# Row directions first in image 0, and a quarter of its front as side steps of its first scans

## The chip, the cores and the metric

The kernel runs on one core of one Trainium2 chip. A core has five engines that are programmed apart from each other: TensorE (PE, with its weight loads as PEld), VectorE (DVE), ScalarE (ACT), GpSimd (POOL) and SyncE (SP), which here issues all transfers between the chip's memory and the core's on-chip buffers; sixteen DMA engines carry them out. The metric is the device time of one launch in microseconds, the median of the runs. Beside it stands one execution taken by the hardware profiler, with the start and the duration of every instruction.

## The reference, cut to what matters

Eight images of 96 channels and 64 x 64 pixels go through a state-space block and an attention block. What concerns this change is the first half of the first block:

```
xn = _ln(shortcut, ln1_w, ln1_b)
xz = jnp.einsum('bhwc,ec->bhwe', xn, in_proj_w)
xw, z = jnp.split(xz, 2, axis=-1)
xc = lax.conv_general_dilated(xc, conv_w, (1, 1), 'SAME', ...)      # 3x3, by channel, 192 channels
xc = _silu(xc + conv_b[None, :, None, None])
s0 = _local_scan(xc, WSZ, False)                                    # 8x8 windows, row by row
s1 = _local_scan(xc, WSZ, True)                                     # the same, column by column
xs = jnp.stack([s0, s1, s0[..., ::-1], s1[..., ::-1]], axis=1)      # four directions
x_dbl = jnp.einsum('bkdl,kcd->bkcl', xs, x_proj_w)                  # step sizes, B and C of each direction
...
def step(hst, inp):
    dA = jnp.exp(dt_i[..., None] * A)
    hst = dA * hst + (dt_i * u_i)[..., None] * b_i[:, :, None, :]
    y = jnp.einsum('bkdn,bkn->bkd', hst, c_i)
```

The scan runs over all 4096 pixels of an image, once in each of four directions: rows forward, rows backward, columns forward, columns backward. Their four outputs are brought back to one order of pixels and added. Norms, gating, two more convolutions, attention and a small feed-forward part follow (the back end).

## The kernel before, in words

An image is cut into NC = 8 chunks of T = 512 pixels. A chunk holds eight rows of the picture, which is one row of 8 x 8 windows.

**The front** (`front`, line 403) makes what the scans read. It has two stages. `normed` (line 415) takes one chunk at a time: layer norm of the input, written to the scratch tensor `xnd`. `paired` (line 451) takes two neighbouring chunks at a time: it loads 18 rows of `xnd` (`im`), makes z with a silu (written to `zd`), the skip part (`base`), the 3 x 3 convolution as nine products a row block (line 435, 27 steps for a pair), a second silu, and writes the result twice: `u[0]` in the order of rows and `u[1]` in the order of columns (line 505 transposes within windows). Last come the products for step sizes, B and C (`xdbl`, lines 513 and 514), written to `xd[0]` and `xd[1]` in the same two orders. In the column order a chunk of pixels touches all eight column chunks, so the first column chunk is whole only when all four pairs are done; in the row order a chunk is whole when its own pair is.

Each stage works on a kit (`front_kit`, line 300), a set of tiles with a PSUM bank of its own. A stage is a generator: between two `yield`s it issues a few instructions, and the number yielded says after how many steps of the kernel's own clock it wants to go on. `side_by_side` (line 844) runs a stage on several kits by turns, each kit with its share of the chunks. For image 0 this is done before anything else, with four kits (f0, f1, y01, y2): line 877.

**The scans.** A unit is one chunk in one direction: 8 images x 4 directions x 8 chunks = 256 units (lines 855 to 868). In each image the pair of column directions (1) comes first, forward and then backward, and then the row directions (0). A unit has 24 slots. In a slot DVE runs one `tensor_tensor_scan` over 128 x 512 (line 1133) and, in 14 of the 24, a product with C (line 1135); ACT makes the decay for two slots ahead (line 1072) and keeps the carry (lines 1136, 1141); POOL makes the inputs (`inputs`, line 952) and multiplies outputs by C (`outputs`, line 958); PE sums over the states (`sums`, line 972). `plan` (line 1007) says in which slot each of these is issued, and also when the loads for coming units are issued on SP: step sizes two units ahead (`fetched_dt`), B and C (`states`), u, and the spreading of delta and du. `gather` (line 993) takes a unit's sum out of PSUM and asks for its write to `y`; a unit reads, in `before` (line 964), what the direction ahead of it has left there. The first direction reads `u` in its place. Going from the column to the row directions, the backward column units write through a transposing copy (line 999) into `y[0]`.

Every engine works through its own queue in the order of issue, and so does SP. Writes are not issued at once: `later` (line 113) holds a request for three steps of the clock.

**Side streams.** While the units of image b run, one step of a side stream may be issued in each slot (`advance`, line 1096). There are two: the front of image b + 1 on kit_f (PSUM bank f0, at a pace of 1.55 slots for each step), and the back end of image b − 1 on kit_b (bank f1, pace 1). While image 0 runs there is no back end, and bank f1 is idle. The back end's first stage, `gated`, takes a chunk only when it is in the image's `done` set, which `gather` fills as the last direction finishes chunk by chunk. Steps that load another function table on ACT wait for slots in which they disturb least (`quiet`, line 392). Before the units of a new image start, the side streams are run to their end (`drained`).

Of the kernel before, what the change touches and what calls it, by code (L numbers as in the profile page):

```python
# [23 lines left out]
NC = L // T  # L24
# [19 lines left out]
def kernel(ctx: ExitStack, tc: tile.TileContext, a, out):  # L44
# [255 lines left out]
    def front_kit(pool, tag):  # L300
        k = Kit()
        k.tag, k.turn = tag, 0
        k.x = [Part(plain(pool, f"{tag}x{i}")) for i in range(2)]
        k.e = [plain(pool, f"{tag}e{i}") for i in range(4)]
        k.pre = pool.tile([P, 3, T], F32, name=tag + "pre")
        k.im = Part(pool.tile([C + 1, 18, W2], F32, name=tag + "im"))
        k.pad = padded(pool, tag + "pad")
        return k
# [535 lines left out]
    def side_by_side(stages, kits):  # L844

        for stage, cs in stages:
            todo = [cs] if cs is None else [cs[i :: len(kits)] for i in range(len(kits))]
            drained(*(Stream(stage(k, c)) for k, c in zip(kits, todo)))
            drained(Stream(settled()))
# [4 lines left out]

    units, images = [], []
    for b in range(out.shape[0]):
        s = {"b": b, "done": set(), "live": b + 1 == out.shape[0]}
        images.append(s)
        for pair in (1, 0):
            for back in range(2):  # L860
                for i in range(NC):
                    u = Unit()
                    u.s, u.pair, u.back, u.k = s, pair, back, pair + 2 * back
                    u.c, u.start = (NC - 1 - i if back else i), i == 0
                    u.new, u.i = (pair, back, i) == (1, 0, 0), len(units)
                    u.bc, u.hb, u.delta, u.du = {}, {}, {}, {}
                    u.banked = BANKED[int(b == 0 or u.i % 32 >= NC)]
                    units.append(u)

    TILES = [(g, j) for g in range(2) for j in range(3)]  # L870

    fp = ctx.enter_context(tc.tile_pool(name="small", bufs=1))
    kit_f = front_kit(wp, "f0")
    first = front(0, images[0])
    with tc.tile_pool(name="begin", bufs=1) as pool:
        table("natural_log_exp_and_others")
        side_by_side(first, [kit_f] + [front_kit(pool, t) for t in ("f1", "y01", "y2")])

    kit_b = back_kit(wp, "f1", False)
    scan_pool = ExitStack()  # L880
    sp = scan_pool.enter_context(tc.tile_pool(name="scan", bufs=2))

# [80 lines left out]

    def before(u):

        src = u.s["u"][1] if u.k == 1 else u.s["y"][u.pair]
        u.plain = []
        for i, rows in enumerate((slice(0, P), slice(P, src.shape[0]))):
            t = sp.tile([P, T], F32, tag=f"u{i}", name=f"u{i}", bufs=1)[: rows.stop - rows.start]
            u.plain.append(into(t, src[rows, bass.ts(u.c, T)]))  # L970

    def sums(u, ns, m):

        if ns[0] == 0 and m == 0:
            u.p = (bank("y01", "p01"), bank("y2", "p2"))
        low, up = slice(0, 64), slice(64, P)
        if len(ns) == 2:
            todo = [(u.p[0][low], ns[0], m), (u.p[0][up], ns[1], m)]
        else:
            todo = [(u.p[1][low], ns[0], 2 * m), (u.p[1][up], ns[0], 2 * m + 1)]  # L980
        for ps, n, i in todo:
            nc.tensor.matmul(  # L982
                ps, halves, u.hb[n][:, i, :], start=TILES[n][0] == 0 and m == 0, stop=False, skip_group_check=True
            )
        if ns[-1] == 5 and m == 1:
            first = u.k == 1
            for ps, w, x in (
                (u.p[0], dd_a if first else ident, u.plain[0]),
                (u.p[1][low] if first else u.p[1], dd_b if first else ident, u.plain[1]),
            ):  # L990
                nc.tensor.matmul(ps, w, x, start=False, stop=True, skip_group_check=True)  # L991

    def gather(u, i):

        ps, d = u.p[i], slice(P * i, P * i + P)
        t = sp.tile([ps.shape[0], T], F32, tag=f"yt{i}", name="yt", bufs=1)
        dst = u.s["y"][1 if u.k == 1 else 0][d]
        if u.k == 3:
            nc.scalar.copy(transposed(t), scanned(ps))
            later(to_columns(dst, u.c), by_window(t))  # L1000
        else:
            nc.scalar.copy(t, ps)
            later(dst[:, bass.ts(u.c, T)], t)
        if u.k == 2 and i == 1:
            u.s["done"].add(u.c)

    def plan(u, last, nxt, third):

# [93 lines left out]
    for u in units:  # L1102
        last, nxt, third = (at_index(u.i + d) for d in (-1, 1, 2))
        if u.new:
            drained(*side)
            b = u.s["b"]
            side = []
            if b:
                side.append(Stream(chain((SETTLE,), in_turn(back_end(b - 1, last.s), kit_b, False))))
            if b + 1 < out.shape[0]:  # L1110
                side.append(Stream(in_turn(front(b + 1, images[b + 1]), kit_f, True), PACE))
            else:
                final = back_end(b, u.s)
                last_kit = back_kit(None, "f0", True, kit_f)
                side.append(Stream(final[0][0](last_kit, range(1, NC)[::-1])))
        if third and third.new:
            drained(*side[-1:])
            all_issued()
        if u.start:
            carry = sp.tile([P, 24], F32, tag="carry", name="carry")  # L1120
        todo = plan(u, last, nxt, third)
        for slot in range(24):
            n, m = divmod(slot, G)
            g, j = TILES[n]
            q, hb, first_at = 24 * u.i + slot, u.hb[n], 0 if u.back else T - 1
            col = carry[:, 8 * j + g * G + m : 8 * j + g * G + m + 1]
            while kept:
                kept.pop(0)()
            decays(q + 2)
            d = da.pop(q)  # L1130
            banked = m < u.banked[n]
            dd, x = (d[:, ::-1], hb[:, m, ::-1]) if u.back else (d, hb[:, m, :])
            nc.vector.tensor_tensor_scan(dd if banked else x, dd, x, 0.0 if u.start else col, ALU.mult, ALU.add)  # L1133
            if banked:
                nc.vector.tensor_tensor(hb[:, m, :], d, u.bc[1, g][:, m, :], ALU.mult)  # L1135
                kept.append(lambda col=col, d=d, at=first_at: nc.scalar.copy(col, d[:, at : at + 1]))  # L1136
            elif m == G - 1:
                lo = 8 * j + g * G
                kept.append(
                    lambda c=carry[:, lo + u.banked[n] : lo + G].unsqueeze(2), h=hb[:, u.banked[n] :, :], at=first_at:  # L1140
                    nc.scalar.copy(c, h[:, :, at : at + 1])  # L1141
                )
            for f, args in todo[slot]:
                f(*args)
            place[0] = slot
            advance(slot)
# [89 lines left out]
```

## Time and profile before

| What | us |
|---|---|
| Median of 3 runs (11326.49 to 11333.61) | 11327.45 |
| Profiled execution, its own time | 11335.55 |
| Its span, first to last instruction | 11333.8 |
| First scan of image 0 starts | 352.6 |
| First scan of image 1 starts | 1640.4 |
| Busy over the span: DVE, POOL, PE, ACT | 10390.3, 10398.8, 8544.5, 7478.7 |

An answer on stretches of time gives, for each stretch, its length, the busy time and the number of instructions (in brackets) of PE, PEld, DVE, ACT and POOL, the share of full clock that PE was granted, the busy share of the DMA engines and what they moved in GB/s. A line of a timeline gives start, length, engine, source line, operation, the tile written and the tile read, the shapes, and how long the engine had been idle and for whom it had waited. SPq is SP's queue: there the length is that of the issue, not of the transfer. "x2" joins two instructions of one kind that follow each other; a product in 32-bit floats appears as two passes.

### The profile page before, as it was taken

To read this page: it belongs to the slowest core of one execution; us is meant where nothing else is said; L and a number is where in the kernel's file an instruction comes from. 1 tells how busy PE (TensorE), PEld (TensorE's weight loads), DVE (VectorE), ACT (ScalarE), POOL (GpSimd) and SP (SyncE) were. 2 spreads that over 40 slices of the span, in tenths; PEclk is the share of its full clock that TensorE was granted. 3 is DMA by queue.
4 is the path that set the end of the run, shared out by engine and by line. 5 is a ranking of instruction groups with operands and counts; after the bars stand their busy time and mean duration, and the time that the engine had idled before them with its cause. 6 is when DMAs were issued, how large, how long until landed. Compare 5 with 4: busy or idle time off the path is not lost. (4 is left out here: it accounts for less than half of the span.)

```text
span 11333.8 us, 97039 instructions
## 1 busy us (share of the span) xinstructions
PE 8544.5 (75%) x23270; PEld 2320.9 (20%) x23270; DVE 10390.3 (92%) x10868; ACT 7478.7 (66%) x14899; POOL 10398.8 (92%) x2783
## 2 busy tenths in 40 slices
PE   6577658887678876888678876788768877676677
PEld 2111112222122211222112221222212221111212
DVE  0799999999999999999999999999999999999993
ACT  3566656767666676667766676666766667666674
POOL 0799999999999999999999999999999999999991
PEclk8678878888788877889788887888878888787788
DMA  2788878898888888888888888889888888888883
GB/s 70 170 197 197 200 188 210 208 226 200 202 207 211 221 198 201 212 212 216 195 212 207 214 217 195 208 205 224 213 197 207 211 220 201 195 199 196 202 199 90
DMA packets 1081040, 2253.25 MB, mean 199 GB/s; under 512 B 419609, under 2 KB 420314, under 8 KB 949395
## 3 DMA queue, kind: packets, MB, share of 16 engines
q1 hardware_dynamic: 1080467, 2247.05, 81.5%
q8 instruction: 184, 3.01, 0.1%
q14 instruction: 389, 3.19, 0.1%
HBM read 1507.14 MB, written 336.69 MB: 163 GB/s over the span
## 5 line engine op out<-in xcount | busy, mean ns | idle before, releaser
L956 POOL TENSOR_TENSOR hb<-b,du 128x2048 f32<-128x2048 f32 x1536 | 6935.8, 4532 | 23.0 <-DMA du<-ua 16.0
L1072 ACT ACTIVATE da<-delta,w_a_logs 128x512 f32<-128x512 f32 x6144 | 4216.4, 689 | 696.7 <-DVE hb L1133 575.6
L982 PE MATMUL p<-hb,halves 128*64 128x512 f32 x12288 | 3813.9, 729 | 809.0 <-POOL hb L962 391.7
L1133 DVE TENSOR_TENSOR_SCAN da<-da,carry,hb 128x512 f32<-128x512 f32 x3087 | 3949.2, 1279 | 57.1 <-ACT da L1072 53.4
L962 POOL TENSOR_TENSOR hb<-hb,c 128x2048 f32<-128x2048 f32 (+2 forms) x768 | 2982.3, 3883 | 304.7 <-ACT carry L1141 262.6
L1133 DVE TENSOR_TENSOR_SCAN hb<-da,carry,hb 128x512 f32<-128x512 f32 x2289 | 2781.1, 1264 | 59.4 <-ACT da L1072 58.4
L1135 DVE TENSOR_TENSOR hb<-da,c 128x512 f32<-128x512 f32 x3528 | 2440.6, 692 | 153.9 <-DVE da L1133 0.9
L1136 ACT COPY carry<-da 128x1 f32<-128x1 f32 x3528 | 554.8, 157 | 2356.0 <-DVE hb L1135 2345.5
L982 PEld LDWEIGHTS p<-hb,halves 128*64 128x64 f32 x12288 | 914.5, 161 | 3556.5 <-issue 2126.2
L435 PE MATMUL conv<-f0im,taps 97*128 97x512 f32 (+1 forms) x2088 | 909.3, 669 | 89.8 <-ACT f0pre L491 50.3
L1133 DVE TENSOR_TENSOR_SCAN da<-da,hb 128x512 f32<-128x512 f32 x441 | 537.8, 1219 | 27.9 <-POOL hb L956 26.5
L938 POOL TENSOR_TENSOR ua<-nat,ua 128x512 f32<-128x512 f32 x256 | 326.7, 1276 | 257.6 <-DMA b<-xd 257.6
L935 DVE SCALAR_TENSOR_TENSOR nat<-dt,nat 128x512 f32<-128x512 f32 x384 | 259.5, 676 | 239.3 <-ACT nat L933 239.3
L921 PE MATMUL dt<-dts,dt_w 7*64 7x512 f32 (+1 forms) x1024 | 450.8, 660 | 18.8 <-DVE nat L935 14.3
L991 PE MATMUL p<-u,ident 128*128 128x512 f32 x768 | 436.0, 695 | 5.3 <-DMA u<-y 5.1
L376 PE MATMUL ctr<-f1b,cen_c 96*96 96x512 f32 x460 | 271.0, 695 | 198.8 <-DVE f1b L770 160.6
L435 PEld LDWEIGHTS conv<-f0im,taps 97*128 97x128 f32 (+1 forms) x2088 | 254.5, 175 | 676.4 <-issue 524.4
L1133 DVE TENSOR_TENSOR_SCAN hb<-da,hb 128x512 f32<-128x512 f32 x327 | 377.9, 1204 | 4.9 <-ACT da L1072 4.9
L382 PE MATMUL var<-f1b,ones_c 96*96 96x512 f32 x346 | 207.9, 685 | 152.6 <-ACT f1b L379 143.0
L1141 ACT COPY carry<-hb 128x4 f32<-128x4 f32 (+2 forms) x768 | 146.7, 191 | 197.3 <-DVE hb L1133 184.8
L656 PE MATMUL cab<-f1m,cab_w 96*96 96x512 f32 x348 | 206.0, 719 | 91.1 <-ACT f1b L665 41.7
L619 PE MATMUL cab<-f1im,cab_w 97*32 97x512 f32 x1044 | 264.7, 627 | 12.8 <-DMA f1im<-xld 7.9
(425 smaller groups left out, 7479.0 us busy)
## 6 DMA issues: line engine op xcount, KB each, us to landing
b<-xd SPq DMA_DIRECT2D x1024, 512.0 KB
c<-xd SPq DMA_DIRECT2D x1024, 512.0 KB
delta<-nat SPq DMA_DIRECT2D x1536, 128.0 KB
du<-ua SPq DMA_DIRECT2D x1024, 128.0 KB
y<-yt SPq DMA_DIRECT2D x512, 256.0 KB
u<-y SPq DMA_DIRECT2D x384, 256.0 KB
ua<-u SPq DMA_DIRECT2D x256, 256.0 KB
du<-ub SPq DMA_DIRECT2D x512, 128.0 KB
```

The source lines that it names most:

```text
L376: nc.tensor.matmul(ps, cen_c, src, start=i == 0, stop=i == len(srcs) - 1)
L435: nc.tensor.matmul(ps, taps[:, t, lo : lo + n], im[:, r0 + dy : r0 + dy + 8, dx : dx + HW], start=t == 0, stop=t == 8,)
L921: nc.tensor.matmul(ps, dt_w[32 * w.k : 32 * w.k + R + 1, d], w.dts, start=True, stop=True)
L938: nc.gpsimd.tensor_tensor(x, u.nat, x, ALU.mult)
L956: nc.gpsimd.tensor_tensor(hb, u.bc[0, g], u.du[j].unsqueeze(1).to_broadcast([P, G, T]), ALU.mult)
L962: nc.gpsimd.tensor_tensor(hb, hb, u.bc[1, TILES[n][0]][:, lo:, :], ALU.mult)
L982: nc.tensor.matmul(ps, halves, u.hb[n][:, i, :], start=TILES[n][0] == 0 and m == 0, stop=False, skip_group_check=True)
L991: nc.tensor.matmul(ps, w, x, start=False, stop=True, skip_group_check=True)
L1072: nc.scalar.activation(da[q], u.delta[j], AF.Exp, scale=a_neg[:, u.k, j, g * G + m : g * G + m + 1])
L1133: nc.vector.tensor_tensor_scan(dd if banked else x, dd, x, 0.0 if u.start else col, ALU.mult, ALU.add)
L1135: nc.vector.tensor_tensor(hb[:, m, :], d, u.bc[1, g][:, m, :], ALU.mult)
L1136: kept.append(lambda col=col, d=d, at=first_at: nc.scalar.copy(col, d[:, at : at + 1]))
```

## The change

Three things are changed, all for image 0 alone.

The order of its directions is turned: rows forward, rows backward, columns forward, columns backward. `u.order` counts the directions of an image from 0 to 3 and takes the place of tests on `u.k`. The copy into the other order of pixels now stands in the second direction (rows backward write into `y[1]`) and in the fourth (columns backward write into `y[0]`). Since a column chunk touches all chunks, image 0's chunks are declared done all at once, at the gather of its last unit.

The paired stage before the scans takes only the first three pairs of chunks (0 to 5), on three kits. The `normed` stage still takes all eight chunks on four kits; the fourth, kit_2, now lies in the pool that stays, and after the first units kit_b uses its tiles in place of tiles of its own.

The fourth pair (chunks 6 and 7) becomes a side stream on kit_2 while the first units of image 0 run, beside the front of image 1. Before unit 4 it is run to its end, if it has not got there.

```diff
-        s = {"b": b, "done": set(), "live": b + 1 == out.shape[0]}
+
+        s = {"b": b, "done": set(), "live": b + 1 == out.shape[0], "pairs": (1, 0) if b else (0, 1)}
...
+        for order, (pair, back) in enumerate((p, k) for p in s["pairs"] for k in range(2)):
...
-    kit_f = front_kit(wp, "f0")
+    kit_f, kit_2 = front_kit(wp, "f0"), front_kit(wp, "f1")
     first = front(0, images[0])
     with tc.tile_pool(name="begin", bufs=1) as pool:
         table("natural_log_exp_and_others")
-        side_by_side(first, [kit_f] + [front_kit(pool, t) for t in ("f1", "y01", "y2")])
-
-    kit_b = back_kit(wp, "f1", False)
+        kits = [kit_f] + [front_kit(pool, t) for t in ("y01", "y2")]
+        (stage, cs), (behind, pairs) = first
+        side_by_side(((stage, cs),), kits + [kit_2])
+        side_by_side(((behind, pairs[:3]),), kits)
+
+    kit_b = back_kit(wp, "f1", False, kit_2)
...
-        src = u.s["u"][1] if u.k == 1 else u.s["y"][u.pair]
+        src = u.s["y" if u.order else "u"][u.pair]
...
-        dst = u.s["y"][1 if u.k == 1 else 0][d]
-        if u.k == 3:
+
+        other = (u.pair, 1 - u.pair, u.pair, 0)[u.order]
+        dst = u.s["y"][other][d]
+        if other != u.pair:
             nc.scalar.copy(transposed(t), scanned(ps))
             later(to_columns(dst, u.c), by_window(t))
...
-        if u.k == 2 and i == 1:
-            u.s["done"].add(u.c)
+        if u.order == 3 and i == 1:
+            if other == u.pair:
+                u.s["done"].add(u.c)
+            elif u.c == (0 if u.back else NC - 1):
+                u.s["done"].update(range(NC))
...
-            if b:
+            if b == 0:
+                side.append(Stream(behind(kit_2, pairs[3:])))
+            else:
                 side.append(Stream(chain((SETTLE,), in_turn(back_end(b - 1, last.s), kit_b, False))))
...
+        if u.i == pairs[3] - 2:
+            drained(side[0])
         if third and third.new:
             drained(*side[-1:])
```

## The prediction

> **What bounds the kernel now.** I read the page, then busy time by stage, then the timelines of the opening, then busy time by unit.
>
> ```profile
> span 11333.8 us, 97039 instructions
> PE 8544.5 (75%) x23270; PEld 2320.9 (20%) x23270; DVE 10390.3 (92%) x10868; ACT 7478.7 (66%) x14899; POOL 10398.8 (92%) x2783
> ```
>
> DVE and POOL bound the span as a whole, but the page's first slice shows them idle. Busy time by stage (stretch, length, busy us of PE, PEld, DVE, ACT, POOL, clock, DMA share, GB/s):
>
> ```profile
> 147.50:240.50 93.00, 92.89 (x288) 37.02 (x287) 0.00 (x0) 8.04 (x13) 0.00 (x0) 1.00 0.02 6
> 270.20:317.20 47.00, 46.23 (x48) 8.14 (x48) 0.00 (x0) 8.43 (x16) 0.00 (x0) 0.50 0.45 110
> 317.20:352.60 35.40, 6.11 (x8) 1.30 (x9) 1.38 (x2) 7.57 (x12) 7.05 (x4) 0.50 0.85 202
> 352.60:1640.40 1287.80, 855.34 (x2248) 228.26 (x2248) 1252.93 (x1272) 798.05 (x1631) 1280.40 (x336) 0.77 0.81 194
> ```
>
> To 317 us the front of image 0 is bound by PE (93 us of convolution at full clock, 47 us of xdbl products at half clock); then come 35 us of loads; from the first scan at 352.6 us image 0 is bound by POOL (1280 of 1288) with DVE beside it, and PE and ACT have room. Work that leaves the opening and needs only PE, ACT and DMA is a candidate gain.
>
> The opening's timeline on ACT, PE and SP (start, length, engine, line, what):
>
> ```profile
> 242.44 1.48 ACT L443 ACTIVATE f0pre<-f0pre 128x1536 f32<-128x1536 f32 x1
> 246.52 1.48 ACT L443 ACTIVATE f1pre<-f1pre 128x1536 f32<-128x1536 f32 x1
> ```
> ```profile
> 270.25 2.00 PE L513 MATMUL xdbl<-f0pre,xp_a 128*80 128x512 f32 x2 [10.12 <-ACT f0e L521]
> 272.18 1.99 PE L514 MATMUL xdbl<-f0pre,xp_b 64*80 64x512 f32 x2
> 274.10 1.99 PE L513 MATMUL xdbl<-f1pre,xp_a 128*80 128x512 f32 x2
> ```
> ```profile
> 317.18 0.30 SPq L121 DMA_DIRECT2D xd<-y2e  x1
> 319.44 0.61 SPq L896 DMA_DIRECT2D dts<-xd  x2
> ```
>
> A silu costs each kit 4.08 us of ACT (two table loads with it), an xdbl set 3.85 us of PE, and SP stands 2 us at the first dts load.
>
> Busy time of the first four units of image 0, and of one unit of image 1, where two side streams run:
>
> ```profile
> 352.60:391.10 38.50, 19.79 (x44) 4.70 (x46) 38.01 (x41) 21.14 (x45) 38.50 (x10) 0.60 0.67 157
> 391.10:432.30 41.20, 28.52 (x74) 6.94 (x70) 40.59 (x44) 27.05 (x58) 41.20 (x12) 0.79 0.77 186
> 432.30:473.00 40.70, 23.31 (x62) 5.62 (x62) 39.97 (x43) 26.25 (x57) 40.70 (x11) 0.82 0.80 192
> 473.00:514.60 41.60, 26.66 (x70) 6.55 (x68) 40.66 (x43) 27.13 (x58) 40.58 (x12) 0.77 0.80 190
> 1678.00:1725.00 47.00, 40.65 (x98) 9.67 (x94) 43.05 (x46) 31.67 (x66) 44.18 (x12) 0.78 0.91 224
> ```
>
> In the first four POOL is busy almost throughout and PE 98 of 162 us. The crowded unit has PE at 86%, and both DVE and POOL lose time: there lies the risk.
>
> **What the Trainium skill says.** TensorE: Matmul & The Clock Gate, "Part 1: The HAM clock gate": the array runs at half clock until some 3.4 us of sustained activity. The trace agrees for the convolution, but the xdbl products kept PE busy 46 of 47 us and stayed at 0.50, so I don't count on a rise there. ScalarE: Activation LUTs, "What ACT_TABLE_LOAD costs": about 1.28 us for the load itself, plus a drain; the trace has 1.28 us, and 4.08 us from one silu to the next.[...]
>
> **The change, part by part.** Removed from the opening: one of four kits in every round of the paired stage (three chunk pairs on three kits). The normed stage keeps four kits.
> - z: the fourth first product (105.97 − 102.78 = 3.2 us) and a quarter of two rounds (107.80 to 116.16, 2.1 us) make 5.3; with cold and warm rounds mixed otherwise I take 4.5 (3.3 to 5.3).
> - silu on z: 4.1.
> - base: rounds from 132.98 to 147.23, a quarter is 3.6.
> - convolution: 147.23 to 240.4, a quarter is 23.3.
> - silu on u: 4.1.
> - column copies: 3 × 1.01 = 3.0 (L505; the xdbl round behind them waits for ACT).
> - xdbl: 12 sets become 9 after 270 us, 3 × 3.85 = 11.6.
> - dts: with rows first, unit 0 reads what kit f0 wrote some rounds earlier, not the last column write of xd, so SP's stop goes: 2.0 (0 to 2).
> Sum 56.2. The 35 us of loads behind it move whole: b and c are issued after the last xd write and move 202 GB/s either way.
>
> Added to image 0's scans: the front of chunks 6 and 7 on kit_2, one step a slot. Its steps are 93 slots of unit 0 to 3 (11 for landing, 9 z, 10 with silu, 8 base, 33 convolution, 2 and 20 after it, up to 12 of quiet waits), so it is over before unit 4 calls for it at slot 96, and that drain costs nothing; unit 6's dts is fetched just after.
> - PE: 44 matmuls' worth (z 3, base 6, convolution 27, xdbl 8), 0.86 us each at full clock (93.1 us / 108) = 38 us. The four units' 98.3 us at clock 0.75 are 73 us at full clock; 111 of 162 fit above clock 0.69.
> - ACT: 3 × 0.6 + 2 × 4.1 + 2 × 0.6 + 3 × 0.7 + 3 × 1.1 + 4 × 0.6 = 19 us, against 102 busy of 162. The decays queue behind these; units of image 0 in which a silu runs show DVE idle 1.6 to 2.2 us against 0.6 to 0.9, so 1 us each, 2 in all.
> - DMA: im, x, zd, base, both u and xd add about 4.2 MB, 26 GB/s over four units on 157 to 192; units at 207 to 216 GB/s (720 to 800 us) still take 40 to 41 us. On SP each write waits for ACT with the next unit's delta, du, b and c behind it; those are issued 9 or more slots (15 us) ahead. Hidden while steps lag less than that.
> - Stalls from a fuller PE (an eviction on ACT waits, decays behind it): no row gives it for this mix. At best 0; at worst the crowded units' excess DVE idle, at most 3.5 us a unit, 14. I take 4, for the two convolution units.
> So side work costs 6 (2 to 16).
>
> Moved: the direction pairs of image 0. Scans, sums and gathers are as many as before. The transposing gathers now stand in orders 1 and 3, so 16 more copies take 1.09 instead of 0.58 us, and their y writes go in 256-byte runs; ACT has the room: 0 (0 to 2). Chunks of image 0 count as done only after its last gather; but the side stream of image 1 starts at slot 12, after that gather's slot 11, as it does now. Its first y load then stands on SP for a y write issued just before: 2 to 4 us, which SP has free there (1663.5 to 1665.6 is idle) and b's lead covers the rest: 0. kit_b takes kit_2's tiles when the front no longer needs them: 0.
>
> Net 56.2 − 6 = 50. On the profiled execution 11335.6 − 50 = 11285 (its span 11333.8 and 1.8 around it); the median of the runs lies 8.1 below it: 11327.5 − 50 = 11277.
>
> **Rivals.** (a) Full clock in xdbl: with a shorter burst before it, PE may keep its clock. 9 sets × (3.85 − 1.72) = 19 more: 11258. Against: the 3.6 us of idle PE behind the convolution (240.4 to 244.0), where the clock fell, stays, and 9 us of column copies follow. (b) Crowded units: side steps cost as in image 1, 14 to 16: 11287. For it: units at 45 to 47 us there; against: those also carry more DVE work, 43 against 40 us. (c) Slower: the clock stays at half through units 0 to 3. PE needs 111 / 0.5 = 222 us in 162; its lag of 60 us holds the evictions on ACT, and with them decays and DVE: −56 + 60 + 6 = +10, 11338. It decides from a clock under about 0.52; before, those units have 0.60 to 0.82, and this very convolution ran at 1.00. (d) The opening is bound by transfers anyway, and the steps taken out change nothing: 11327. Against: DMA share 0.02 and 0.45 in the two PE stretches.
>
> **From numbers to chances.** Likeliest case 0.70 (own range 11268 to 11288, from the bounds of z, dts and the stalls); (a) 0.10; (b) 0.15, tail to 11300; (c) 0.03; (d) 0.02. The range 11255 to 11298 holds the first, most of (a) and (b). A difference under 0.2% (23 us) can hardly be told from none: faster 0.95, same 0.04 (c, d), slower 0.01 (c with more lag behind it).
>
> **What would show it.** The first scan near 296 us, 56 earlier; convolution 70 us long with three kits; 9 xdbl sets 3.85 us apart (1.7 would be a); dts directly behind the last xd issue. Units 0 to 3 together 162 + 6; DVE idle up by 1 to 2 us a unit, PE over 85% of them. From image 1 on every unit as before. Wrong if the first scan comes as forecast and units 0 to 3 grow by over 16 us, or if image 1's first units grow, where the late "done" would be the cause.

## The result, and the profile after

The changed kernel takes 11288.08 us, median of 5 runs (11276.69 to 11299.44); the kernel before took 11327.45 beside it (11322.44 to 11333.61). The ratio is 0.9964, with an interval of 0.9951 to 0.9976. A second sample on another chip gave 11278.56 (11275.63 to 11292.27) against 11334.86, a ratio of 0.9956 (0.9943 to 0.9968). The forecast was 11277 with a range of 11255 to 11298. The profiled execution was the quickest of the first sample, 11276.69 (forecast for it: 11285).

The page of the changed kernel, span and busy time:

```profile
span 11274.7 us, 97032 instructions
PE 8525.3 (76%) x23270; PEld 2313.7 (21%) x23270; DVE 10391.9 (92%) x10868; ACT 7482.6 (66%) x14899; POOL 10398.6 (92%) x2782
```

DVE and POOL are busy as long as before (10390.3 and 10398.8) and PE nearly so (8544.5); it is the span around them that is shorter. Busy time by stage of the changed kernel: convolution of the opening, last nine xdbl sets, loads, and the units of image 0 (columns as in the prediction: stretch, length, PE, PEld, DVE, ACT, POOL, clock, DMA share, GB/s):

```profile
137.00:206.00 69.00, 68.94 (x215) 27.37 (x213) 0.00 (x0) 5.51 (x9) 0.00 (x0) 1.00 0.01 5
228.50:264.10 35.60, 34.69 (x36) 6.11 (x36) 0.00 (x0) 6.32 (x12) 0.00 (x0) 0.50 0.43 106
264.10:299.20 35.10, 6.11 (x8) 1.28 (x8) 1.43 (x3) 7.57 (x12) 7.10 (x4) 0.50 0.89 208
299.20:1592.10 1292.90, 890.42 (x2356) 241.00 (x2356) 1253.59 (x1273) 820.57 (x1652) 1280.93 (x336) 0.78 0.82 196
```

Convolution and xdbl have each lost a quarter, the loads are as long as before, the first scan starts at 299.2 instead of 352.6, and image 0 takes 5.1 us more. The opening's timelines on ACT, PE and SP, changed kernel:

```profile
207.98 1.48 ACT L443 ACTIVATE f0pre<-f0pre 128x1536 f32<-128x1536 f32 x1
212.07 1.48 ACT L443 ACTIVATE y01pre<-y01pre 128x1536 f32<-128x1536 f32 x1
```
```profile
228.67 2.00 PE L513 MATMUL xdbl<-f0pre,xp_a 128*80 128x512 f32 x2 [7.08 <-ACT f0e L521]
230.60 1.99 PE L514 MATMUL xdbl<-f0pre,xp_b 64*80 64x512 f32 x2
232.52 2.00 PE L513 MATMUL xdbl<-y01pre,xp_a 128*80 128x512 f32 x2
```
```profile
264.05 0.30 SPq L121 DMA_DIRECT2D xd<-y2e  x1
264.40 1.13 SPq L899 DMA_DIRECT2D dts<-xd  x2
266.36 0.35 SPq L906 DMA_DIRECT2D ua<-u  x1
267.92 1.23 SPq L893 DMA_DIRECT2D b<-xd  x2
```

A silu still costs 4.09 us a kit, an xdbl set 3.85 us at half clock. The first dts load stands directly behind the last xd write, as forecast; a stop on SP, 0.8 us long, is now at the load behind it (264.40 + 1.13 = 265.53, and ua at 266.36).

The first four units of image 0 in the changed kernel:

```profile
299.20:337.60 38.40, 22.45 (x54) 5.45 (x56) 37.92 (x41) 22.52 (x48) 38.40 (x10) 0.67 0.75 176
337.60:379.10 41.50, 38.91 (x92) 9.92 (x88) 40.76 (x43) 32.02 (x64) 41.50 (x12) 0.88 0.81 200
379.10:419.80 40.70, 36.69 (x125) 10.36 (x126) 39.96 (x42) 27.51 (x59) 40.70 (x11) 1.00 0.83 206
419.80:464.30 44.50, 33.85 (x90) 7.82 (x86) 40.95 (x44) 35.84 (x68) 40.65 (x12) 0.81 0.85 220
```

Units 1 and 2, which carry the moved convolution, have PE busy for 94% and 90% of their time and are hardly longer than before (41.2 and 40.7). Only unit 3 has grown clearly, from 41.6 to 44.5. What happens there is on DVE and ACT (timelines of the changed kernel; the bracket is the idle time and who ended it):

```profile
429.48 0.68 DVE L424 TENSOR_TENSOR f0pad<-f0e,var 96x512 f32<-96x512 f32 x1 [1.00 <-ACT var L370]
447.99 0.68 DVE L424 TENSOR_TENSOR f0pad<-f0e,var 96x512 f32<-96x512 f32 x1 [1.81 <-ACT var L370]
```
```profile
421.46 1.28 ACT L398 ACT_TABLE_LOAD   x1
422.75 1.48 ACT L443 ACTIVATE f1pre<-f1pre 128x1536 f32<-128x1536 f32 x1
424.25 1.28 ACT L398 ACT_TABLE_LOAD   x1
...
427.18 1.11 ACT L505 COPY f1e<-f1pre 128x512 f32<-128x512 f32 x1
428.19 0.65 ACT L369 ACTIVATE var<-var,eps 96x512 f32<-96x512 f32 x1
428.87 0.57 ACT L370 ACTIVATE var<-var 96x512 f32<-96x512 f32 x1
...
446.24 0.56 ACT L518 COPY f1e<-xdbl 80x512 f32<-80x512 f32 x1
446.70 0.65 ACT L369 ACTIVATE var<-var,eps 96x512 f32<-96x512 f32 x1
447.38 0.57 ACT L370 ACTIVATE var<-var 96x512 f32<-96x512 f32 x1
```

f1 is the moved quarter, f0 the front of image 1. The quarter's silu, with its two table loads, and a column copy (L505) stand on ACT ahead of the two activations of image 1's layer norm (L369, L370). Their consumer on DVE, L424, comes next in DVE's queue, which runs in order: DVE stands for 1.00 us, with the scans behind it. The second stop, 1.81 us where the kernel before has 0.33, comes 18 us later, when the silu is long over. This time copies of the quarter's xdbl results (L518 above, another at 440.12) and the step sizes of a coming unit stand ahead of the norm; that these copies make the difference is read from ACT's order, not tested. DVE's idle time in this unit is 3.55 us, 0.94 in the kernel before.

Span against span: the first scan comes 53.4 us earlier, image 0 grows by 5.1, images 1 to 7 are 7.0 shorter in sum and the end behind the last scan 3.7 shorter, 59.0 in all. Only the first two can be put down to the change. Images 3 to 6 take between 1343 and 1350 us each from one kernel of this study to the next, the tail 240 to 247, though no kernel touches them. The second sample's profile has the first scan at 304.9, image 0 at 1293.1, and a span of 11287.9.

### The profile page after: what moved, and what is told of

Its sections match the earlier page's. It is cut to its first block, busy times and chain, and to the rows that moved or that the text cites. A ratio compares the mean times of both kernels' runs of the same rounds, so it can differ in the third digit from the quotient of the medians.

```text
span 11274.7 us, 97032 instructions
## 1 busy us (share of the span) xinstructions
PE 8525.3 (76%) x23270; PEld 2313.7 (21%) x23270; DVE 10391.9 (92%) x10868; ACT 7482.6 (66%) x14899; POOL 10398.6 (92%) x2782
## 5 line engine op out<-in xcount | busy, mean ns | idle before, releaser
L376 PE MATMUL ctr<-f1e,cen_c 96*96 96x512 f32 x402 | 234.7, 693 | 137.4 <-DVE f1e L770 98.6
L382 PE MATMUL var<-f1e,ones_c 96*96 96x512 f32 x350 | 210.8, 687 | 146.3 <-ACT f1e L379 131.7
```

## The experiments

No kernel leaves a part of the computation out. Some do more: one computes chunks 6 and 7 twice, two give xdbl wider weights, and the four filled ones issue products that nothing reads. A diff is against the changed kernel, in 8, 9, 11 and 12 against the experiment that is carried on; "..." marks lines left out.

**1. The order alone.** All four pairs before the scans, no side stream, only the order of the directions turned.

```diff
-        side_by_side(((behind, pairs[:3]),), kits)
+        side_by_side(((behind, pairs),), kits + [kit_2])
...
-            if b == 0:
-                side.append(Stream(behind(kit_2, pairs[3:])))
-            else:
+            if b:
...
-        if u.i == pairs[3] - 2:
-            drained(side[0])
```

> The directions of image 0 turned, and nothing else: all four pairs of the front before the scans on four kits, no side front. My theory: turning the order is worth almost nothing by itself. SP's 2 us stop at the first dts load goes, but the loads of B and C behind it last as long, so the first scan starts at 351 to 352.5 us (352.6 before); the transposing gathers in the last eight units of image 0 cost 1 to 2 us in image 0, which lasts 1289 to 1290 us (1287.8 before). Device time within 4 us of before. Rival: the turned order is a gain or a loss of its own, through earlier loads (first scan before 348 us) or through the late mark of done chunks (units 0 to 3 of image 1 longer by more than 2 us together).

Measured: 11324.39 us (13 runs) against 11330.84 (26 runs), ratio 0.9997 (0.9988 to 1.0005). First scan at 352.1 (before: 352.6), image 0 1288.9 us (1287.8), the first four units of image 1 37.9, 45.6, 44.4 and 43.6 us, before 37.9, 46.7, 44.7 and 43.6. SP's queue in this kernel:

```profile
317.91 0.30 SPq L121 DMA_DIRECT2D xd<-f1e  x1
318.27 0.82 SPq L899 DMA_DIRECT2D dts<-xd  x2
319.26 0.35 SPq L906 DMA_DIRECT2D ua<-u  x1
```

The stop in front of dts is gone, yet from the last xd write to the first scan 34.1 us pass instead of 35.4: 0.7 of the 2 us are lost again in the loads that follow. The turned order by itself can't be told from no change, and the late "done" costs image 1 nothing.

**2. The side work alone.** The order and the side stream as in the change, but the opening also does all four pairs; the quarter is computed twice.

```diff
-        side_by_side(((behind, pairs[:3]),), kits)
+        side_by_side(((behind, pairs),), kits + [kit_2])
```

> As the changed kernel, but all four pairs are also computed before the scans on four kits; the side stream then computes the front of chunks 6 and 7 a second time, to the same values. So the opening is as long as before and the side work is there: the price of the side work alone. My theory, from the changed kernel's trace: about 3 us in units 0 to 4, nearly all in unit 3 (44 us instead of 41.6), units 1 and 2 as before although PE is filled there, and 1 to 2 us in the last eight units; first scan at 351 to 352.5 us, device time 3 to 8 us above before. Rival, as predicted blind: 6 us in units 0 to 3 with most of it in the convolution's units 1 and 2. Rival of the crowded units: 14 us.

Measured: 11335.62 us (13 runs), ratio 1.0002 (0.9994 to 1.0010). Image 0 takes 1293.0 us, 4.1 more than with the order alone; the first five units are 38.4, 41.6, 40.7, 44.4 and 41.0, as in the changed kernel. So the side work costs 4 us with the long opening as with the short one, and the rest of the change is what the opening loses. The medians of the two kernels lie 11 us apart, with intervals that overlap.

**3. The changed kernel again**, with no edit, as a second sample.

> The changed kernel once more, with more executions than its first comparison had. Its profiled execution was 59 us under before, its median 39. The stages say 53 us less up to the first scan and 5 us more in image 0, so 48. Theory: 48 is what the change does, and the rest is scatter between executions in images 1 to 7; a larger sample gives a ratio of 0.9955 to 0.9962 (43 to 51 us). Rival: the profile's images 3 to 7 (11 us shorter) belong to the change: 0.9950 or less.

Its time is given above. Its ratio lies in the range of the theory, but the interval doesn't shut the rival's 0.9950 out. Its units are 38.4, 41.7, 40.7, 44.4 and 41.0: unit 3 is no accident of one execution. But its first scan stands 5.7 us later. Busy time in one stretch of the base stage, first in the changed kernel's profile, then in that of the second sample:

```profile
119.60:136.00 16.40, 13.83 (x31) 4.48 (x31) 0.00 (x0) 8.63 (x10) 0.00 (x0) 1.00 0.43 137
```
```profile
119.60:136.00 16.40, 15.69 (x18) 4.39 (x18) 0.00 (x0) 7.86 (x8) 0.00 (x0) 0.50 0.43 136
```

One program, two executions: full clock from 119.6 us in one, only from 136.0 in the other, where PE was busy for 96% of these 16 us. That is where the 5.7 us are.

**4. Image 1's front held back.** If unit 3 suffers from two fronts on one ACT, it should recover when image 1's front starts later, at a quicker pace.

```diff
-                side.append(Stream(in_turn(front(b + 1, images[b + 1]), kit_f, True), PACE))
+                ahead = in_turn(front(b + 1, images[b + 1]), kit_f, True)
+                side.append(Stream(chain((68,), ahead), 1.4) if b == 0 else Stream(ahead, PACE))
```

> As the changed kernel, but the front of image 1 waits for 95 slots, until the side front of chunks 6 and 7 is done, and then goes at 1.4 slots a step instead of 1.55, so that it ends in time. It tells what unit 3 of the changed kernel pays for (44.4 us, 41.6 before). Theory: two streams meet; DVE, in its own order, stands at the norm product of image 1's front, which waits for its two ACT functions, which stand behind the silu and the column copies of the side front. Then without that norm unit 3 takes 41 to 42 us and DVE is idle under 1.8 us in it, and units 0 to 2 are 1 to 2 us shorter together (no norm product on DVE). Rival: the silu and the column copies alone hold the decays; unit 3 stays at 43.5 us or more. Device time 0 to 6 us below the changed kernel's in the first case, unless the quicker front costs that later.

Measured: 11286.69 us (4 runs), ratio 0.9962 (0.9948 to 0.9976). Unit 3 of this kernel:

```profile
421.90:463.70 41.80, 33.87 (x84) 7.63 (x80) 39.76 (x42) 31.48 (x60) 41.80 (x12) 0.75 0.88 221
```

Unit 3 falls from 44.4 to 41.8, with POOL busy throughout; DVE's idle time falls from 3.55 to 2.04, not quite to what was expected. Units 0 to 3 take 159.5 us, against 165.0 with both fronts in them and 162.0 in the kernel before, which has only image 1's. So the quarter alone is no dearer than image 1's front alone: either leaves unit 3 at 41.6 to 41.8, both together make it 44.4. That they meet on ACT is what the timelines above show. These sums alone would also fit two costs that merely add, since no kernel has neither front in these units. The held front gives the gain back later (image 0: 1293.8), so this is a diagnosis, no cure.

**5. and 6. Wider products in xdbl.** The xdbl products use 80 columns of the array and, every second one, 64 rows. If the number of columns kept the clock at half, 128 of them should lift it (the 64 rows stay as they are): once padded with zeros (the first two added lines in the loop), once with copies of real columns (the next two, in their place).

```diff
+        for n, t in (("a", xp_a), ("b", xp_b)):
+            wide[n] = pool.tile([P, 2, P], F32, name="wide_" + n)
+            nc.vector.memset(wide[n], 0.0)
+            nc.vector.tensor_copy(wide[n][:, :, :XP], t)
...
+            nc.vector.tensor_copy(wide[n][:, :, :XD], t[:, :, :XD])
+            nc.vector.tensor_copy(wide[n][:, :, XD:P], t[:, :, : P - XD])
...
-                        nc.tensor.matmul(ps, xp_a[:, p, :], pre[:, q, :], start=True, stop=False)
+                        nc.tensor.matmul(ps, wa[:, p, :], pre[:, q, :], start=True, stop=False)
```

> As the changed kernel, but in the opening the xdbl products have weights of 128 columns, the upper 48 zero; same instructions, same streamed columns, only the first 80 rows are used. It asks why PE stayed at half clock there for 36 us of unbroken products. Theory: the clock follows how much of the array works, and 80 of 128 columns with 64 of 128 rows every second time is too little; then with 128 columns the clock rises after some microseconds, xdbl sets go from 3.85 to 1.7 us, the first scan comes 8 to 17 us earlier (282 to 291 us). Rival: the width plays no part (zeros do no work, or something else holds the clock); sets stay at 3.85 us and the first scan at 299 us.

> As the one with xdbl weights of 128 columns, but the upper 52 columns hold copies of the lower ones instead of zeros, so that the whole width does real work. With zeros the sets stayed at half clock. Theory: zeros count as no work, and with real numbers in all columns the clock rises during the products; sets fall to 1.7 us. Rival: the width has no part in it, and sets stay at 4.0 us.

Measured: 11283.39 us (5 runs, ratio 0.9961, 0.9948 to 0.9974) and, in one run, 11270.3; first scans at 304.0 and 301.2. In both, the sets take 4.01 us and the clock stays at 0.50 to the end. PE in the zero-padded kernel:

```profile
213.66 2.08 PE L516 MATMUL xdbl<-f0pre,wide_a 128*128 128x512 f32 x2 [3.58 <-ACT f0pre L445]
...
232.81 2.08 PE L516 MATMUL xdbl<-f0pre,wide_a 128*128 128x512 f32 x2 [6.92 <-ACT f0e L525]
```

The theory of the columns fell; the 64 rows were not tested. The brackets point at what is left: idle PE ahead of the products.

**7. Idle time filled, in part.** Products that nothing reads stand behind the convolution (2 a kit) and behind each kit's first xdbl set (3).

```diff
+        def busy(im, n):
+            if place[0] is None:
+                ps = bank("dt", "busy")
+                for _ in range(n):
+                    nc.tensor.matmul(ps, taps[:, 0, 0:P], im[:, 0:8, 0:HW], start=True, stop=True)
...
                 silu(pre)
+                busy(im, 2)
...
+                        if p == q == 0:
+                            busy(im, 3)
```

> As the changed kernel, with products of the convolution's shape, whose results nobody reads, issued where PE would stand idle in the opening: two for each kit ahead of the first xdbl products, three for each behind them. Theory: PE's clock fell because it stood idle for 3.6 us after the convolution and for 7 us during the column copies; without these gaps it stays at full speed through the xdbl products, whose sets take 1.7 instead of 3.85 us, and the first scan comes 15 to 19 us earlier (280 to 285 us). Rival: products of xdbl's kind can't hold the clock; it falls some microseconds after the last filler, and the first scan is at 292 us or later.

Measured: 11287.54 us (4 runs), ratio 0.9960 (0.9946 to 0.9973), first scan at 304.9; the rival's number came in. (The base stage of this execution came back to full clock only at 137.2, as late as in the second sample, whose first scan is also at 304.9: against that one nothing was gained.) But PE shows that its reason is another (partly filled kernel):

```profile
223.31 1.02 PE L520 MATMUL xdbl<-y01pre,xp_a 128*80 128x512 f32 x2
...
235.62 1.43 PE L520 MATMUL xdbl<-f0pre,xp_a 128*80 128x512 f32 x2 [2.86 <-ACT f0e L530]
236.97 1.99 PE L521 MATMUL xdbl<-f0pre,xp_b 64*80 64x512 f32 x2
```

The first sets ran at full clock, 1.02 us instead of 2.00. Then 2.86 us of idle PE were left, and 0.6 us after them the clock fell and stayed down.

**8. The gap filled whole.** Five products in place of three.

```diff
-                            busy(im, 3)
+                            busy(im, 5)
```

> As the one with filled gaps, with five instead of three fillers behind each kit's first xdbl products, so that PE has no idle time left between the end of the convolution and the second group of xdbl products (2.9 us were left, and the clock fell there). It tells the gap from the kind of work. Theory: the gap alone did it; the clock stays at 1.00 through the nine sets, 1.7 us each, and the last of them ends 14 to 19 us earlier than with three fillers, measured from the end of the convolution. Rival: xdbl's products can't hold the clock; it falls to 0.5 within some 10 us of the last filler and most sets take 3.85 us.

Measured, one run: 11266.41 us, below all ten runs of the changed kernel. That alone proves little, since the one run of experiment 6, which gained nothing in the opening, lies below them too; the trace decides. The first scan is at 282.4, in an execution whose base stage came back to full clock at 119.4, as in the changed kernel's first profile (119.6, first scan 299.2). PE in this kernel, and the busy time of the stretch:

```profile
226.15 4.56 PE L445 MATMUL busy<-y2im,taps 97*128 97x512 f32 x10
230.55 1.02 PE L520 MATMUL xdbl<-f0pre,xp_a 128*80 128x512 f32 x2
231.50 1.08 PE L521 MATMUL xdbl<-f0pre,xp_b 64*80 64x512 f32 x2
232.51 1.08 PE L520 MATMUL xdbl<-y01pre,xp_a 128*80 128x512 f32 x2
```
```profile
229.00:250.00 21.00, 19.81 (x40) 4.37 (x39) 0.00 (x0) 5.59 (x10) 0.00 (x0) 1.00 0.70 170
```

With no gap, all nine sets run at full clock, 2.03 us each. From the end of the convolution to the end of the last set it takes 43.2 us, 57.4 in the changed kernel and 56.9 in the partly filled one. So it is the idle PE ahead of xdbl that costs the clock; xdbl's own products hold it.

**9. Fillers behind every set**, to see if the products need help to hold the clock.

```diff
-                        if p == q == 0:
-                            busy(im, 5)
+                        busy(im, 5 if p == q == 0 else 1)
```

> The same, with one more filler behind every later xdbl set. If xdbl's products can't hold the clock by themselves: with a filler of full size in every third of the time the clock stays at 1.00, a set with its filler takes 2.6 us, and the nine of them 23 instead of 35 us. Rival: a third isn't enough, the clock falls, and a set with its filler takes 5.5 us, 50 us for nine.

Measured, one run: 11276.51 us, first scan at 292.0. A set with its filler takes 2.93 us, nine of them 8 us more than without. They need no help to hold the clock.

**10. Two pairs in the opening.** If a pair that leaves the opening costs only 4 us later, a second one should too. Chunks 0 to 3 are done before, on two kits; chunks 4 and 5 run on kit_2, with 30 steps issued under the loads; 6 and 7 on kit_f ahead of image 1's front.

```diff
+        ahead = [Stream(behind(k, [c])) for k, c in zip(kits, pairs)]
+        third_pair, fourth_pair = Stream(marked(kit_2, 2)), marked(kit_f, 3)
...
+    for _ in range(EARLY):
+        tick()
+        third_pair.run()
     fetched_u(units[1])
...
+                if b == 0:
+                    coming = chain(fourth_pair, (SETTLE,), (1.4 * n for n in coming))
...
```

> The change carried one step further: only chunks 0 to 3 are taken before the scans, on two kits; chunks 4 and 5 run on kit_2 (30 of their steps while the first loads of B and C are under way, the rest in units 0 and 1), chunks 6 and 7 on kit_f in units 0 to 3, and the front of image 1 starts after that, at 1.4 slots a step. Theory: the opening is bound by PE in proportion to the pairs taken there, so the first scan comes another 50 us earlier (246 to 252 us), and units 0 to 3, which have PE and ACT to spare, lose 5 to 15 us: device time 35 to 45 us below the changed kernel. Rival: with two streams from the start PE and ACT are full, image 0 loses 25 us or more, and the gain is under 25 us.

Measured: 11249.48 us (5 runs) against 11334.86, ratio 0.9927 (0.9913 to 0.9940), where the changed kernel has 0.9956 (0.9943 to 0.9968) beside it: faster than both, though the two intervals nearly touch. It is 29 us below the changed kernel, where 35 to 45 were expected: the first scan was expected at 246 to 252 and came at 260.1; image 0 takes 1300.7 us. ACT in this kernel:

```profile
243.39 0.58 ACT L485 COPY f1e<-base 96x512 f32<-96x512 f32 x1 [5.76 <-PE base L482]
255.19 0.69 ACT L492 ACTIVATE f1pre<-conv,cb_a 128x512 f32<-128x512 f32 x1 [11.22 <-PE conv L436]
258.19 0.60 ACT L948 ACTIVATE nat<-dt 128x512 f32<-128x512 f32 x1 [2.32 <-PE dt L940]
...
259.36 1.90 ACT L1096 ACTIVATE da<-delta,w_a_logs 128x512 f32<-128x512 f32 x3
```

The transfers were done by 249.5 us. But among the early steps is the eviction of the side convolution (ACT's copy of the result out of PSUM), and the first decays (L1096) stand behind it in ACT's queue: 11.22 us of waiting that the order makes.

**11. Fewer early steps**, 20 instead of 30, and a denser pace in units 0 and 1.

```diff
-EARLY = 30
+EARLY = 20
...
-        third_pair, fourth_pair = Stream(marked(kit_2, 2)), marked(kit_f, 3)
+        third_pair, fourth_pair = Stream(marked(kit_2, 2), 0.7), marked(kit_f, 3)
...
+        if u.i < 2:
+            third_pair.run()
```

> As the one with two pairs before the scans, but only 20 steps of the third pair are issued ahead of the scans (up to its skip part, no convolution), and the rest at 0.7 slots a step in units 0 and 1. There the first scan came at 260 us, because ACT stood 11 us at the eviction of a convolution that ran at half clock, with the step sizes of unit 1 and the first decays behind it. Theory: without it the first scan comes at 247 to 250 us; units 0 and 1 lose some of that, being fuller; device time 4 to 10 us under the first version. Rival: what is moved only stalls units 0 and 1 instead, image 0 grows by as much as the first scan gains, and the device time is the same within 3 us.

Measured: 11254.85 us (5 runs), ratio 0.9934 (0.9920 to 0.9947); first scan at 260.6, units 0 and 1 at 49.7 each, where experiment 10 has 44.2 and 43.9; image 0 grows to 1310.9. The expected gain failed to come: nothing at the first scan, and the denser pace costs the units 11 us (the intervals of the two kernels overlap). PE and ACT of this kernel say why the first scan stayed:

```profile
248.40 9.10 PE L436 MATMUL conv<-f1im,taps 97*128 97x512 f32 x14 [0.67 <-ACT f1e L485]
257.43 1.12 PE L940 MATMUL dt<-dts,dt_w 7*128 7x512 f32 x2
```
```profile
258.64 0.60 ACT L948 ACTIVATE nat<-dt 128x512 f32<-128x512 f32 x1 [10.29 <-PE dt L940]
```

The eviction had gone from ahead of the first decays, but seven products of the convolution were still ahead of unit 1's dt on PE, and ACT waited for that one with the decays behind it. The order was mended on one engine only.

**12. Both findings together.** Experiment 10 with the fillers of 8, and with twelve of the early steps issued behind the first decays, two in a slot, so that no convolution is ahead of them on any engine.

```diff
-    for _ in range(EARLY):
+    for _ in range(EARLY - 12):
...
+        if u.i == 0:
+            third_pair.pace = 0.5 if n < 12 else 1.0
+            third_pair.run()
```

> Two findings put together on the two-pair opening. First, the idle PE in front of xdbl is filled by products that nothing reads (two ahead, five behind the first set of each kit). Second, where the two-pair run had ACT stand 11.2 us at the first convolution eviction of the third pair, with the first decays behind it in its queue, twelve of the thirty early side steps are now issued behind the first decays, two a slot in the first twelve slots of unit 0. My theory: 8 xdbl sets at 2.0 in place of 3.85 us bring the last one some 12.5 us forward (14.4 were measured for nine), to about 200 us, the transfers then take some 37 us as in the two-pair run, ACT is not held, and the first scan starts at 236 to 241 in place of 260.1. Units 0 and 1 together 88 to 94 us. Device time 11226 to 11236. Rival: ACT's decays for the slots after the first are held at the same eviction, and the units give back what the first scan gains from the second finding: first scan near 240, units 0 and 1 together over 97, device 11238 to 11245. Second rival: the idle gap is not closed with two kits, and xdbl stays at half clock: first scan at 249 to 253.

Measured: 11234.83 us (5 runs, 11223.55 to 11244.05) against 11334.92, ratio 0.9915 (0.9901 to 0.9929). ACT and POOL:

```profile
239.02 0.60 ACT L957 ACTIVATE nat<-dt 128x512 f32<-128x512 f32 x1 [0.52 <-DMA du<-ub]
239.64 0.63 ACT L959 ACTIVATE nat<-nat 128x512 f32<-128x512 f32 x1
240.18 1.90 ACT L1105 ACTIVATE da<-delta,w_a_logs 128x512 f32<-128x512 f32 x3
```
```profile
238.03 8.97 POOL L984 TENSOR_TENSOR hb<-b,du 128x2048 f32<-128x2048 f32 x2 [16.82 <-DMA du<-ua]
```

ACT no longer stands, and the first scan, at 242.6, waits for POOL, which waited for du: the transfers bind again, as in the changed kernel (from the last xdbl copy to the first scan it is 35.5 us here and 35.7 there, 47.9 in experiment 10). It missed its forecast of 236 to 241 for two reasons. The convolution ended 5.0 us later than in experiment 10 (178.3 and 173.3), since the base stage of this execution came back to full clock later (128.1 and 117.2), the scatter of experiment 3. And the stretch from there to the last xdbl copy shrank by 10.1 us (38.9 to 28.8), not 12.5: the fourteen fillers take 12.8 us of it (182.13 − 178.27 and twice 4.46) for six later sets, where the three kits had nine. Units 0 and 1 take 87.1 us, 88.1 in experiment 10. This version has the lowest median: it lies 100.1 us below that of the kernel before, and its interval lies clear of both intervals of the changed kernel. Against experiment 10 the intervals overlap.

## Why the prediction was right

The time was forecast at 11277, and the two samples gave 11288 and 11279. The forecast's mechanism stands: the opening is shorter by about 50 (53.4 and 47.7 in the two profiles of the changed kernel, 56.2 forecast), image 0 longer by about 5. The nearness of the sum has some luck in it: the opening gave less than forecast, and the side work cost less too. Step by step, as the start of the next stage moved in the first profile:

| Step | forecast | cumulative: forecast | measured |
|---|---|---|---|
| z | 4.5 | 4.5 | 3.75 |
| silu on z | 4.1 | 8.6 | 7.8 |
| base | 3.6 | 12.2 | 11.3 |
| convolution | 23.3 | 35.5 | 34.5 |
| silu on u | 4.1 | 39.6 | 38.5 |
| column copies | 3.0 | 42.6 | 41.6 |
| xdbl | 11.6 | 54.2 | 53.1 |
| dts, at its issue | 2.0 | 56.2 | 55.0 |
| dts, at the first scan | | 56.2 | 53.4 |

- **The quarters of the opening** were right to within 1 us each in this profile. This works because every stage of the opening but the loads is bound by PE or ACT with kits taking turns; a stage's length is then kits times one kit's work. In the second profile all stages from the convolution on are as long, but the convolution starts 6.0 us later.
- **dts** is the term that fell short. Its load did move by 55.0 us, but b by 53.8 only (321.72 to 267.92), since SP then stopped at ua, and the loads behind are bound by transfers (DMA share 0.89). 0.3 us of the 2.0 reached the first scan here, 1.3 in experiment 1; in ten profiles of kernels with the turned order and three or four pairs in the opening, the stretch from the last xd write to the first scan lies between 32.9 and 35.4 us (35.4 before), so its worth is not known better than that. That an instruction is issued earlier was taken as a gain without asking if a transfer-bound stretch behind it starts earlier.
- **The side work** was put at 6. Units 0 to 3 grew by 3.1 and image 0 by 5.1, of which 1.1 come with the order and 4.1 with the steps (experiments 1 and 2). The load on PE was right: its busy time times its clock rose by some 39 us in these units (an estimate from the lines shown; forecast 38). The size of the cost was about right and the place wrong. "I take 4, for the two convolution units" failed: those units grew by 0.3 us together, with PE busy for over 90%. The forecast tied the cost to a full PE; in fact most of it sits in unit 3, where PE has room, and it goes when image 1's front is held back (experiment 4), as it would if ACT's order makes it. The "1 each" for the silus holds neither: the first silu cost DVE nothing, and in unit 3 DVE lost 2.6 us, 1.0 of it right behind the second silu and its column copy. The count of steps left no room either: 93 slots and up to 12 of quiet waits are more than the 96 there are. In the trace it was enough, with the quarter's last xdbl copy at 457.07, in unit 3.
- **PE over 85%** and **DVE idle up by 1 to 2 us in each of the four units** were both wrong as signs: PE has 131.9 of 165.1 us, 80%, and DVE's idle time rose by 2.6 us in unit 3 and by 0.13 or less in units 0 to 2.
- **Rival (a), full clock in xdbl**, was rejected for the right reason: the forecast said that the idle PE behind the convolution, and then the column copies, would keep the clock down. Experiment 8 shows it, by taking the gaps away: first scan at 282.4, 16.8 us earlier, where the rival had 19.
- **Rival (c)** did not come near its point: units 0 to 3 have the clock at 0.67, 0.88, 1.00 and 0.81; its threshold was 0.52. With more PE work the clock was higher in all four (before: 0.60, 0.79, 0.82, 0.77).
- **Rival (d)** and the late "done": transfers are 35 us of the opening, in both kernels; image 1's first units are unchanged.
- **What the forecast left out** is the spread. The opening of one program differs by 5.7 us between two executions, with the return of the clock in the base stage. In the five profiles with three kits and no fillers the first scan lies between 299.2 and 304.9, in the three with four kits between 350.0 and 352.6. With three kits the base stage has more idle PE between its products, which may be why; that is argued, not shown. Nor is it shown that the times spread more: the changed kernel's first five runs span 23 us and those before 11, but the 26 runs of the kernel before beside experiment 1 span 32.

## What to carry to other kernels

Work that moves from a serial opening under a loop with a slack engine costs little as long as no in-order queue puts it ahead of what the loop needs next: look at each queue for the first instruction behind the moved step, not at the engine's busy share. An earlier issue in front of a transfer-bound stretch is worth less than it looks (0.3 and 1.3 of 2.0 us). Useless products in idle time of PE pay only if they close the gap: fifteen that left 2.86 us open took 0.5 us off the stretch behind the convolution, and six more, some 5 us of PE, took off another 13.7, because a long run of products follows.

## What the runs showed of the hardware

The clock of PE is asymmetric for these 32-bit products. From half clock, 34.7 us of almost unbroken xdbl products (changed kernel) or 46 us (before) did not raise it, with 80 columns or with 128; from full clock, the same products held it for 18 us. The Trainium skill (TensorE: Matmul & The Clock Gate, "Part 1: The HAM clock gate") has some 3.4 us of sustained activity bring the full clock, with a run-to-run variation of half a microsecond. The convolution, which the forecast named as agreeing, doesn't show it: it starts at full clock. Here it took over 16 us more in one execution of the base stage than in another, and in xdbl it never came; the measurement decides.

The same page warns of gaps (section "HAM oscillation — how this bites in real kernels": none longer than about 3.4 us). Here less was enough: with a gap of 2.86 us the clock was lost, with none it held, and a gap of 2.12 us in the base stage of the changed kernel (before 124.13) did no harm. The traces show more of the pattern. In the first 340 us of all fourteen profiles the granted clock changes only on a grid of 3.41 us. Each of its 52 falls there ends a step of this grid in which PE was busy for at most 58%; in the 528 steps that ended at full clock as they began, PE was busy for at least 49%. So, in these openings, what counts is how much of one step is idle: the 2.12 us were shared by two steps, while the 2.86 us fell almost wholly into one. That step of the partly filled kernel and the next (PE busy 0.62 of 3.41 us, then the lower clock):

```profile
232.83:236.24 3.41, 0.62 (x2) 0.22 (x2) 0.00 (x0) 3.41 (x6) 0.00 (x0) 1.00 0.97 289
236.24:239.65 3.41, 3.41 (x5) 0.68 (x4) 0.00 (x0) 0.87 (x2) 0.00 (x0) 0.50 0.91 224
```

Why the products of the base stage and of the convolution regain the clock (the side convolution of experiment 10 does at 250.3) and those of xdbl do not, these runs leave open: it is not the number of columns, and not zeros in the weights.
